# Loading the first element's blocks four rows to a partition, with its turned blocks written by Pool's queue

## The chip, the cores and the metric

The kernel runs on one core of one Trainium2 chip. The metric is the device time of one execution in microseconds, lower is better. TensorE (PE) multiplies matrices, VectorE (DVE) and ScalarE (ACT) work elementwise, GpSimd (POOL) does elementwise work in on-chip memory (SBUF), and transfers between SBUF and DRAM are issued by SP, ACT or Pool.

## The reference

Two layers over x of shape (8, 256, 96, 96), fp32. Each is a group norm, an operation and a residual.

```
# layer 0, on xn = groupnorm(x), per element b
q_f, k_f, v_f = fft2(w1 xn + b1), fft2(w2 xn + b2), fft2(w3 xn + b3)
attn = normalize(q_f) @ normalize(k_f)^T * temperature     # 8 heads of 32 channels, over 9216 frequencies
attn = softmax(real(attn)) + 1j * softmax(imag(attn))
x = x + w_out @ abs(ifft2(attn @ v_f))
# layer 1, on xn = groupnorm(x)
q, k, v = softplus(Wq xn + bq), softplus(Wk xn + bk), Wv xn + bv
x = x + (q @ (k^T v)) / (q @ sum(k))
```

## The kernel before

The Fourier transforms are not computed. What the attention of layer 0 needs of x are channel-by-channel sums of even and odd combinations of pixels with their mirror images, and the imaginary part of attn acts on an image that is mirrored and rotated along a table R. For each of the eight elements the program has these stages:

- **pair sums** (`pair_sums`): a row h of the image is paired with its mirror row. For 48 rows in 12 units (u = 0 to 11) of four rows each (G = 4), and a thirteenth for the middle row, `turn_blocks(u)` brings channels into the free dimension with DVE's 32x32 stream transposes, `pair(u)` makes sums and differences (tile eo), and `products` multiplies these on PE into two accumulators (acc), 24 matmuls a unit.
- **attention** (`attention`): a chain of small steps that makes the matrix mz.
- **rotation** (`rotate`): 49 steps that multiply the turned rows by pieces of R and write the result y. Its inputs come back from DRAM: xtd (turned blocks) and rx (R).
- **images** (`images`) forms the complex image, its absolute value, and the output projection; **layer1** and **output** do layer 1.

In the program the stages of element b are woven with the pair sums, the attention and the rotation of element b + 1, so that PE always has work. Only element 0 has nothing to be woven with: its pair sums start when the program starts. Its loop is at the end of the kernel:

```python
        for i, _ in enumerate(sums):
            if i > 3:
                next(parts, None)
            if i > 20 and i % 2 == 0:
                fetch()
            if i > 26:
                next(turns)
```

A pair-sum unit yields once per third of its products, so i is 1 + 3u + q. `parts` is the generator `tables`, which builds R and then the small constants, `fetch` loads one row pair of xtd (and R's piece where a new one begins), `turns` makes one rotation step.

The order on each engine is written by hand: within the manual schedule, the instructions of PE, DVE, Pool, SP and ACT run in the order in which the program emits them. Semaphores carry the data dependencies. The transfers of SP and ACT share eight completion lanes, in turn: a transfer also waits until the one eight before it on its lane is complete.

Memory: two arenas of 128 partitions x 2 channel halves (k) x 9232 floats take turns as x (`x_of(b)`) and y (`y_of(b)`). While the pair sums of element b run, its x arena holds no x yet but stages blocks. `load_grouped(b, v)` loads block v (0 to 5, two units each; 6 is the middle row): 32 channels of a group times four sets of two rows on 128 partitions, f the rows and g their mirror rows, in half k = v % 2; eight transfers of 192 KB, with one cut in two for block 0. `turn_blocks(u)` transposes f (unit 2v + r uses the r-th row) and the reversed g into the turned buffer, which begins at TO in both halves. After the second unit of a block it issues on SP the write of the turned block (1.5 MB) to xtd and then the load of block v + 2 (L372 and the lines after it). There is one turned buffer. At r = 0 two small copies (L364, L365) move a column of g by one row, the wrap.

`tables` writes 96 rows of a cosine table to DRAM (rt), reads them back as the long rows of R in 384-byte pieces (`big`, L270), and writes R to rx cut into 13 pieces with overlapping ends (L279, L280), from which `load_r` (L608) fetches one piece per four rows.

Of the kernel before, what the change touches and what calls it, by code (L numbers as in the profile page):

```python
# [52 lines left out]
F32 = mybir.dt.float32  # L53
# [4 lines left out]
P = 128  # L58
# [4 lines left out]
TR = 4  # L63
# [10 lines left out]
def two_layer_kernel(ctx: ExitStack, tc: tile.TileContext, x, w1t, b1, w2t, b2, w3, b3, wot, temp,  # L74
# [49 lines left out]

    SG = NB8 * 2 * W
    TO = 2 * SG + 4

    def staged(b, v, at=0):

        return x_of(b)[:, v % 2, at * SG:at * SG + SG + at]  # L130

    def turned(b):

        return [x_of(b)[:, c, TO:TO + 2 * NQ * C].rearrange("p (q r n) -> p q r n", q=NQ, r=2) for c in range(2)]

    def load_grouped(b, v):

        xs = x[b].rearrange("(c i) h w -> i c h w", i=32)
        if 2 * v == NG:
            m = H // 2  # L140
            f, g = (staged(b, v, i)[:, 0:C].rearrange("p (c w) -> p c w", c=NB8) for i in range(2))
            for q in range(NQ):
                s = slice(32 * q, 32 * q + 32)
                n = 32 if q else 31
                o = W + 1 - 32 * (q + 1)
                nc.sync.dma_start(out=f[s], in_=xs[:, :, m, s])
                nc.sync.dma_start(out=g[s, :, 0:n], in_=xs[:, :, m, o:o + n])
            return
        f, g = (staged(b, v, i)[:, 0:SG].rearrange("p (c w) -> p c w", c=NB8) for i in range(2))
        for a in range(G):  # L150
            h, s = 2 * (G * v + a), slice(32 * a, 32 * a + 32)
            nc.sync.dma_start(out=f[s], in_=xs[:, :, h:h + 2].rearrange("p c r w -> p c (r w)"))
            if h:
                nc.sync.dma_start(out=g[s], in_=xs[:, :, H - h - 1:H - h + 1].rearrange("p c r w -> p c (r w)"))
            else:
                nc.sync.dma_start(out=g[s, :, 0:W], in_=xs[:, :, H - 1])
                nc.sync.dma_start(out=g[s, :, W:2 * W], in_=xs[:, :, 0])

    setup = y_of(0)[:, 0, :]
    t0 = setup[0:H, 0:6 * W]  # L160
    nc.scalar.dma_start(out=t0[:, 0:2 * W], in_=tmat[0, :, W:3 * W])
    for v in range(2):
        load_grouped(0, v)


    ident = const.tile([P, P], F32, name="ident")
# [22 lines left out]
    nc.scalar.dma_start(out=gavg_sb, in_=gavg)  # L189
    gri = setup[:, 6 * W:6 * W + 2 * P]  # L190
    nc.scalar.dma_start(out=gri, in_=gmat)

    pw = const.tile([P, 1], F32, name="pw")
    nc.vector.memset(pw, 1.0)
# [49 lines left out]
    rt = dram.tile([H, 2 * W], F32, name="rt")  # L244
    NP = NG
    RW = TR * (W + 2) + P - W
    rx = dram.tile([NP + 1, W, RW], F32, name="rx")

    xtd = dram.tile([2, NG // 2, P, 2 * NQ * C], F32, name="xtd")
    xtm = dram.tile([W, C], F32, name="xtm")  # L250
# [1 line left out]
    def tables():  # L252

        pcs = ps_tile("pcs")
        for c in range(2):
            nc.tensor.matmul(pcs[0:H, c:c + 1], lhsT=csn[0:1, c, :], rhs=ones[0:1, 0:1], start=True, stop=True)
        cs = t0[:, 5 * W:5 * W + 2]
        nc.vector.tensor_copy(cs, pcs[0:H, 0:2])
        r0 = t0[:, 2 * W:3 * W]
        nc.vector.tensor_scalar_mul(t0[:, 0:W], t0[:, 0:W], cs[:, 0:1])  # L260
        nc.vector.scalar_tensor_tensor(r0, in0=t0[:, W:2 * W], scalar=cs[:, 1:2], in1=t0[:, 0:W], op0=ALU.mult, op1=ALU.add)
        for i in range(2):
            o = (3 + i) * W
            nc.vector.tensor_copy(t0[:, o:o + 1], r0[:, 0:1])
            nc.vector.tensor_copy(t0[:, o + 1:o + W], r0[:, W - 1:0:-1])
        nc.scalar.dma_start(out=rt, in_=t0[:, 3 * W:5 * W])
        big = y_of(0)[0:W, 1, 0:(N + 1) * (W + 2) + P - W]
        rows = big[:, 0:(N + 1) * (W + 2)].rearrange("p (r w) -> p r w", r=N + 1)
        v = rt[0:N + 1, 1:]
        nc.scalar.dma_start(out=rows[:, :, 1:W + 1], in_=bass.AP(v.tensor, v.offset, [[1, W], [2 * W, N + 1], [1, W]]))  # L270
        nc.scalar.copy(rows[:, :, 0:1], csn[0:W, 2, 0:N + 1].unsqueeze(2))
        nc.scalar.mul(rows[:, :, W + 1:W + 2], csn[0:W, 2, 0:N + 1].unsqueeze(2), -1.0)
        nc.scalar.copy(big[:, (N + 1) * (W + 2):], csn[0:W, 2, 0:P - W])
        yield
        for q in range(NQ):
            s = slice(32 * q, 32 * q + 32)
            v = big[s, 0:NP * TR * (W + 2)]
            src = bass.AP(v.tensor, v.offset, [list(v.ap[0]), [TR * (W + 2), NP], [1, RW]])
            nc.scalar.dma_start(out=rx[0:NP].rearrange("i (j q) w -> q j i w", q=NQ)[q], in_=src)  # L279
        nc.scalar.dma_start(out=rx[NP][:, 0:P + 2], in_=big[:, N * (W + 2):N * (W + 2) + P + 2])  # L280
        yield
        for j in range(4):
            o = HEAD * j
            nc.vector.tensor_copy(gsel[:, 0:16, j], gri[:, o:o + 16])
            nc.vector.tensor_copy(gsel[:, 17:32, j], gri[:, P + o + 1:P + o + 16])
            nc.vector.tensor_copy(gsel[:, 32, j:j + 1], gri[:, o + 16:o + 17])
        nc.vector.reduce_sum(rep4[:, 0:D], ident.rearrange("p (j d) -> p d j", d=D), axis=AX.X)
        for j in range(1, 4):
            nc.vector.tensor_copy(rep4[:, 32 * j:32 * j + 32], rep4[:, 0:D])
        nc.vector.tensor_copy(sel8.rearrange("p (i d) -> p i d", d=D), rep4[:, 0:8].unsqueeze(2).to_broadcast([P, 8, D]))  # L290
        nc.vector.tensor_scalar_mul(csn[:, 0:2, N + 1:H], csn[:, 0:2, N + 1:H], -1.0)
        yield from load_small()
# [42 lines left out]
    def pair_sums(b):  # L335
# [9 lines left out]
                                     rhs=eo[0:np_, q, c, m * (P + 1):C + 1 + m], start=(first and m == 0), stop=last,  # L345
                                     skip_group_check=True)

        wrap = two.tile([P, 2 * NB8], F32, tag="wrap", name=f"wrap_{b}")

        def turn_blocks(u):  # L350

            v, r = divmod(u, 2)
            t = turned(b)
            if u == NG:
                f, g = (staged(b, v, i)[0:W, 0:C].rearrange("p (c w) -> p c w", c=NB8) for i in range(2))
                nc.vector.tensor_copy(g[0:32, :, 31:32], f[0:32, :, 0:1])
                for i, src in enumerate((f, g[:, :, ::-1])):
                    nc.vector.transpose(out=t[i][0:W, 0, 0].rearrange("p (c i) -> p c i", c=NB8), in_=src)
                nc.sync.dma_start(out=xtm, in_=t[0][0:W, 0, 0])
                return  # L360
            f = staged(b, v, 0).rearrange("p (c r w) -> p c r w", c=NB8, r=2)
            if r == 0:
                g = staged(b, v, 1)
                nc.vector.tensor_copy(wrap, g[:, 0:SG:W])  # L364
                nc.vector.tensor_copy(g[:, W:SG + 1:W], wrap)  # L365
            o = SG + (1 - r) * W + 1
            g = x_of(b)[:, v % 2, o:o + SG].rearrange("p (c n) -> p c n", c=NB8)[:, :, W - 1::-1]
            for i, src in enumerate((f[:, :, r], g)):
                nc.vector.transpose(out=t[i][:, :, r].rearrange("p q (c i) -> p q c i", c=NB8),  # L369
                                    in_=src.rearrange("p c (q w) -> p q c w", q=NQ))  # L370
            if r:
                nc.sync.dma_start(out=xtd[:, v].rearrange("c p m -> p c m"), in_=x_of(b)[:, :, TO:TO + 2 * NQ * C])  # L372
                if v + 2 <= NG // 2:
                    load_grouped(b, v + 2)

        def pair(u):

            eo = ring_tile(f"eo_{b}_{u}").rearrange("p (q c n) -> p q c n", q=NQ, c=2)
            nq, np_ = (NQ, P) if u < NG else (1, W)
            ft, gt = (t[0:np_, 0:nq, u % 2] for t in turned(b))  # L380
            e, o = (eo[0:np_, 0:nq, c, 1:C + 1] for c in range(2))
            nc.gpsimd.memset(eo[0:np_, 0:nq, :, 0:CB:CB - 1], 1.0 if u < NG else R2)  # L382
            if u == 0:
# [215 lines left out]
    def rotate(b):  # L599
# [5 lines left out]
        def load_r(i):  # L605
            tm = tm_tile(f"tm_{b}_{i}")
            o = (TR if i < NP else 1) * (W + 2) + P - W
            nc.sync.dma_start(out=tm[:, 0:o], in_=rx[i][:, 0:o])  # L608
            return tm

        order = [(c, h, h // TR) for h in range(0, N, 2) for c in range(2)] + [(0, N, NP)]
        area = x_of(b)
        slots = [area[0:W, k, o + 4 * C * i:o + 4 * C * (i + 1)].rearrange("p (c m) -> p c m", c=2)
                 for k, o, n in ((0, LO, 3), (1, LO, 3), (0, LO + 12 * C, 1)) for i in range(n)]
        assert LO + 16 * C <= AW and LO + 12 * C <= LO + NS * CH + 2 * CH
        xts, tms = {}, {}
        at_ = [0]
# [1 line left out]
        def fetch():  # L619
# [9 lines left out]
            if h == N:  # L629
                nc.sync.dma_start(out=xts[i][:, 0, 0:C], in_=xtm)  # L630
            else:
                v, a = divmod(i, G)
                nc.sync.dma_start(out=xts[i], in_=xtd[:, v, 32 * a:32 * a + 32].rearrange("c j (q m) -> (j q) c m", q=NQ))

        def step(i):
# [20 lines left out]
        def steps():  # L656

            for i in range(len(order)):
                while at_[0] < min(i // 2 + len(slots) - 1, len(order) // 2 + 1):
                    fetch()  # L660
                step(i)
                if i >= 24 and i % 8 == 0 and i // 8 < 6:
                    load_x(b, i // 8 - 3)
                yield

        return fetch, steps()

# [347 lines left out]
    with tc.manual_schedule(engines={E.PE, E.DVE, E.Pool, E.SP, E.Activation}):  # L1015
# [1 line left out]
        next(parts)  # L1017
        fetch, turns = rotate(0)
        for i, _ in enumerate(sums):
            if i > 3:  # L1020
                next(parts, None)
            if i > 20 and i % 2 == 0:
                fetch()
            if i > 26:
                next(turns)
        finish(mix(0, attention(0), turns))
        for b in range(B):
# [60 lines left out]
```

## Time and profile before

| | us |
|---|---|
| median of 3 runs | 2651.48 (2646.25 to 2654.46) |
| profiled execution | 2650.85 |
| its span, first to last instruction | 2649.0 |
| PE busy | 2509.3 (95%) |
| DVE, ACT, POOL busy | 1789.0, 1155.9, 865.6 |
| mean granted PE clock | 0.984 |
| pair-sum products of element 0, first to last | 16.0 to 127.7 |
| first image product of element 0 (L710) | 180.31 |

The page gives busy times and, in 40 slices of 66 us, busy tenths of each engine. PE's busy time counts pipelined matmuls, so that a full PE says that matmuls followed one another, not that the array was at its peak. A wait line reads: engine, line and tile that waited, "<-", what ended the wait, then the total in us, how often, and the longest. A line of the order of time reads: start, duration, engine, line, operation, tiles, count, and in brackets the idle time before it with what ended it. SPq and ACTq are the DMA-issuing parts of SP and ACT; the duration of an issue is not that of the transfer.

### The profile page before, as it was taken

What the parts mean: (1) busy time and instruction counts of PE and PEld (TensorE: products, weight loads), DVE (VectorE), ACT (ScalarE), POOL (GpSimd) and SP (SyncE); (2) the same over time, 40 slices, a digit from 0 to 9 for tenths busy, and PEclk for the clock granted to TensorE, in tenths of its full rate; (3) what the DMA queues carried; (4) which work ended last, traced back from release to release, by engine and by line L of the source; (5) the groups of instructions that cost most, each with busy time, mean ns of one, the idle gap of its engine ahead of it and who ended that gap; (6) DMA issues with size and microseconds to landing.
All of it is one profiled execution on the core that took longest, in us unless ns stands there. A gap on an engine that the chain in (4) does not pass through costs nothing. (4 is left out here: it accounts for less than half of the span.)

```text
span 2649.0 us, 41157 instructions
## 1 busy us (share of the span) xinstructions
PE 2509.3 (95%) x15580; PEld 1730.2 (65%) x15580; DVE 1789.0 (68%) x3449; ACT 1155.9 (44%) x1985; POOL 865.6 (33%) x817
## 2 busy tenths in 40 slices
PE   3799999999999999999999999999999999999987
PEld 3775666757677576766668566685666757667544
DVE  3457866577756777568675686757866678766766
ACT  0035353453634526344353544435354353534554
POOL 2213514136042451324422343223523135141311
PEclk8899999999999999999999999999999999999999
DMA  9872628637195461935629264492636826286003
GB/s 210 238 216 60 166 71 270 205 67 189 40 313 161 106 173 57 315 120 143 153 90 305 80 167 129 159 316 42 166 89 230 245 60 179 58 289 210 1 7 144
DMA packets 282797, 413.27 MB, mean 156 GB/s; under 512 B 40772, under 2 KB 208872, under 8 KB 282600
## 3 DMA queue, kind: packets, MB, share of 16 engines
q1 hardware_dynamic: 274304, 406.16, 53.2%
q10 hardware_dynamic: 8296, 4.49, 0.8%
q8 instruction: 123, 2.02, 0.3%
q14 instruction: 74, 0.61, 0.1%
HBM read 256.72 MB, written 153.86 MB: 155 GB/s over the span
## 5 line engine op out<-in xcount | busy, mean ns | idle before, releaser
L710 PE MATMUL z<-arena,mz 128*128 128x384 f32 (+1 forms) x2304 | 593.4, 491 | 0.0
L718 PE MATMUL po<-e,wo 128*128 128x384 f32 x1536 | 527.6, 487 | 1.7 <-ACT e L755 1.7
L754 POOL TENSOR_TENSOR e<-e 128x768 f32<-128x768 f32 x192 | 348.4, 1815 | 552.7 <-ACT e L753 529.3
L343 PE MATMUL acc<-eo 128*128 128x257 f32 (+2 forms) x2368 | 437.1, 336 | 50.0 <-POOL eo L382 23.0
L343 PEld LDWEIGHTS acc<-eo 128*128 128x128 f32 (+1 forms) x2368 | 383.8, 194 | 143.9 <-issue 42.4
L710 PEld LDWEIGHTS z<-arena,mz 128*128 128x128 f32 (+1 forms) x2304 | 310.5, 164 | 236.0 <-issue 51.9
L718 PEld LDWEIGHTS po<-e,wo 128*128 128x128 f32 x1536 | 290.0, 190 | 204.7 <-ACT e L755 7.2
L749 DVE TENSOR_TENSOR e<-z,xT 128x768 f32<-128x768 f32 x384 | 361.9, 950 | 75.4 <-PE z L710 74.9
L647 PEld LDWEIGHTS y<-tm,arena 96*128 96x128 f32 x3072 | 365.9, 195 | 52.9 <-issue 18.9
L647 PE MATMUL y<-tm,arena 96*128 96x128 f32 x3072 | 385.7, 281 | 15.3 <-DMA arena<-xtd 6.4
L753 ACT ACTIVATE e<-e 128x1536 f32<-128x1536 f32 x192 | 284.5, 1482 | 195.2 <-DVE e L749 193.3
L391 POOL TENSOR_TENSOR eo<-arena 128x768 f32<-128x768 f32 x88 | 184.5, 2096 | 536.3 <-DVE arena L369 473.2
L720 DVE TENSOR_TENSOR arena<-arena,po 128x384 f32<-128x384 f32 x384 | 209.9, 553 | 190.0 <-PE po L718 190.0
L755 ACT ACTIVATE e<-e 128x768 f32<-128x768 f32 x192 | 162.0, 844 | 367.1 <-POOL e L754 363.2
L986 POOL TENSOR_TENSOR arena<-arena,po 128x384 f32<-128x384 f32 x180 | 179.1, 1014 | 224.0 <-ACT po L985 224.0
L369 DVE STREAM_TRANSPOSE arena<-arena 128x768 f32<-128x768 f32 x192 | 175.7, 953 | 32.5 <-DMA xtd<-arena 23.0
L299 DVE BATCH_NORM_STATS2 st<-arena 128x6 f32<-128x384 f32 x384 | 194.4, 548 | 0.0
L654 ACT COPY ys<-y 128x4 f32<-128x4 f32 (+1 forms) x200 | 32.4, 162 | 363.8 <-DVE arena L653 363.7
L878 PE MATMUL xT<-ident,arena 128*128 128x128 f32 x1152 | 148.4, 277 | 10.0 <-ACT xT L881 9.6
L878 PEld LDWEIGHTS xT<-ident,arena 128*128 128x128 f32 x1152 | 127.2, 142 | 32.0 <-issue 13.6
L985 ACT COPY po<-o 128x384 f32<-128x384 f32 x180 | 79.0, 485 | 157.4 <-PE o L977 152.4
L653 DVE COPY arena<-y 128x384 f32<-128x384 f32 (+1 forms) x200 | 109.1, 546 | 40.8 <-PE y L647 38.6
(225 smaller groups left out, 2493.1 us busy)
## 6 DMA issues: line engine op xcount, KB each, us to landing
xtd<-arena SPq DMA_DIRECT2D x48, 1536.0 KB
arena<-xtd SPq DMA_DIRECT2D x192, 384.0 KB
arena<-in_x_dram SPq DMA_DIRECT2D x96, 768.0 KB
out_dram<-arena SPq DMA_DIRECT2D x192, 384.0 KB
arena<-in_x_dram SPq DMA_DIRECT2D x376, 192.0 KB
tm<-rx SPq DMA_DIRECT2D x96, 159.0 KB
wl<-in_w1t_dram SPq DMA_DIRECT2D x8, 256.0 KB
wl<-in_w2t_dram SPq DMA_DIRECT2D x8, 256.0 KB
```

The costliest lines, as they stand in the source:

```text
L299: nc.vector.bn_stats(out=st[:, k, c, :], in_=x_of(b)[:, k, c * CH:(c + 1) * CH])
L343: nc.tensor.matmul(acc[c][:, m * (C + 1):m * (C + 1) + C + 1 - m * P], lhsT=eo[0:np_, q, c, 1 + m * P:1 + (m + 1) * P], rhs=eo[0:np_, q, c ...
L391: nc.gpsimd.tensor_add(e, ft, gt)
L647: nc.tensor.matmul(pu[:, o:o + P], lhsT=xt[:, s, k * P:(k + 1) * P], rhs=tm[:, n:n + P], start=True, stop=True)
L710: nc.tensor.matmul(out[:, 0:CH].rearrange("p (h q) -> p h q", q=PR), lhsT=columns(mz, k, c, j), rhs=yz[:, k, f, :, o:o + PR], start=(k == ...
L718: nc.tensor.matmul(po[:, 0:CH], lhsT=wo[:, k, m * P:(m + 1) * P], rhs=e[:, k, :], start=(k == 0), stop=(k == KC - 1))
L720: nc.vector.tensor_add(x[:, m, n], x[:, m, n], po[:, 0:CH])
L749: nc.vector.tensor_add(e[:, 2 * c:2 * c + 2, :].rearrange("p t (q h) -> p t q h", h=H), pz[:, 0:CH].rearrange("p (h q) -> p q h", h=H).uns ...
L753: nc.scalar.activation(e, e, AF.Square)
L754: nc.gpsimd.tensor_add(e[:, 0:2, :], e[:, 0:2, :], e[:, 2:4, :])
L878: nc.tensor.transpose(pt[:, j * C + k * P:j * C + (k + 1) * P], x[:, k, o:o + P], ident)
L986: nc.gpsimd.tensor_add(x[:, m, r], x[:, m, r], t)
```

## The change

For element 0 alone (all others keep their way):

- a block group is four rows of x per partition: three groups (v = 0, 2, 4) of eight 384 KB transfers instead of six blocks of eight 192 KB. Groups 0 and 1 are staged in the two halves of the x arena, group 2 in half 0 of the y arena, the middle row in half 1 of it. All three groups are loaded ahead of everything else; the middle row is loaded after unit 9.
- the turned blocks have two places, T4 and T4 + 2*NQ*C, used in turn by v, and the write to xtd is issued by Pool instead of SP.
- R is written to DRAM in 96 long rows (and a small tile rxm for the last piece); `load_r` reads its piece out of the long rows.
- the parts of `tables` are drawn at i = 1, 6 and from 7 on, instead of from 4 on; the fetches begin at i = 18 instead of 22 and the rotation steps at i = 29 instead of 27.
- the eight places of the fetched rows lie under the staged groups (there were seven, elsewhere in the arena); x for the images' third piece, load_x(0, 2), is loaded after the rotation instead of at its step 40.

```diff
+    S4 = 2 * SG
+    T4 = 2 * S4 + 4
+    def part_of(b, v, o, n):
+        if b:
+            return x_of(b)[:, v % 2, o:o + n]
+        if 2 * v == NG:
+            return y_of(b)[:, 1, H // 2 * W + H // 4 * HB + o:H // 2 * W + H // 4 * HB + o + n]
+        V = v // 2
+        return x_of(b)[:, V, o:o + n] if V < 2 else y_of(b)[:, 0, 10 * W + o:10 * W + o + n]
+    def turned(b, v):
+        o = TO if b else T4 + v % 2 * 2 * NQ * C
+        return x_of(b)[:, :, o:o + 2 * NQ * C]
...
-            h, s = 2 * (G * v + a), slice(32 * a, 32 * a + 32)
-            nc.sync.dma_start(out=f[s], in_=xs[:, :, h:h + 2].rearrange("p c r w -> p c (r w)"))
+            h, s = 2 * G * v + n * a, slice(32 * a, 32 * a + 32)
+            nc.sync.dma_start(out=f[s], in_=xs[:, :, h:h + n].rearrange("p c r w -> p c (r w)"))
...
-    for v in range(2):
-        load_grouped(0, v)
+    load_grouped(0, 0)
...
+    for v in (2, 4):
+        load_grouped(0, v)
...
-    rx = dram.tile([NP + 1, W, RW], F32, name="rx")
+    rx = dram.tile([W, RL], F32, name="rx")
+    rxm = dram.tile([W, P + 2], F32, name="rxm")
...
+        yield
-        big = y_of(0)[0:W, 1, 0:(N + 1) * (W + 2) + P - W]
+        big = y_of(0)[0:W, 1, 0:RL]
...
-            nc.scalar.dma_start(out=rx[0:NP].rearrange("i (j q) w -> q j i w", q=NQ)[q], in_=src)
-        nc.scalar.dma_start(out=rx[NP][:, 0:P + 2], in_=big[:, N * (W + 2):N * (W + 2) + P + 2])
+            nc.scalar.dma_start(out=rx.rearrange("(j q) w -> q j w", q=NQ)[q], in_=big[32 * q:32 * q + 32])
+        nc.scalar.dma_start(out=rxm, in_=big[:, N * (W + 2):N * (W + 2) + P + 2])
...
-            if r:
-                nc.sync.dma_start(out=xtd[:, v].rearrange("c p m -> p c m"), in_=x_of(b)[:, :, TO:TO + 2 * NQ * C])
-                if v + 2 <= NG // 2:
+            if u % 2:
+                (nc.sync if b else nc.gpsimd).dma_start(out=xtd[:, v].rearrange("c p m -> p c m"), in_=turned(b, v))
+                if b and v + 2 <= NG // 2 or v + 2 == NG // 2:
                     load_grouped(b, v + 2)
...
+        places = ((0, LO, 3), (1, LO, 3), (0, LO + 12 * C, 1)) if b else ((0, T4 - 16 * C, 4), (1, T4 - 16 * C, 4))
...
-                v, a = divmod(i, G)
+                v, a = divmod(i, G) if b else (i // 8 * 2 + i % 2, i % 8 // 2)
...
-                if i >= 24 and i % 8 == 0 and i // 8 < 6:
+                if i >= 24 and i % 8 == 0 and i // 8 < 6 and (b or i < 40):
                     load_x(b, i // 8 - 3)
                 yield
+            if b == 0:
+                load_x(b, 2)
...
-            if i > 3:
+            if i in (1, 6) or i > 6:
                 next(parts, None)
-            if i > 20 and i % 2 == 0:
+            if i > 17 and i % 2 == 0:
                 fetch()
-            if i > 26:
+            if i > 28:
                 next(turns)
```

## The prediction

> **What bounds the kernel now.** I read the page's slices first, then the busy time by window, then the waits, and last the order of time of the first 110 us. The page shows where time can be had at all:
>
> ```profile
> PE   3799999999999999999999999999999999999987
> ...
> PEclk8899999999999999999999999999999999999999
> ```
>
> TensorE is full from the third slice on (a slice is 66 us); only the first two have holes, and there the granted clock is 0.8. All that the diff touches for element 0 runs in these two slices. The same in windows of 20 us (columns: window, length, PE, weight load, DVE, ACT, POOL busy with counts, granted clock, DMA share, GB/s):
>
> ```profile
> 0.00:20.00 20.00, 4.75 (x16) 4.14 (x17) 9.77 (x39) 2.05 (x5) 4.24 (x62) 1.00 1.02 191
> 20.00:40.00 20.00, 9.80 (x48) 8.54 (x47) 8.12 (x24) 0.00 (x0) 6.31 (x7) 0.78 1.11 287
> 40.00:60.00 20.00, 7.13 (x40) 6.29 (x38) 3.70 (x8) 0.00 (x0) 0.39 (x1) 0.76 0.52 159
> 60.00:80.00 20.00, 10.84 (x52) 9.53 (x53) 9.10 (x12) 0.00 (x0) 8.59 (x7) 0.76 0.97 215
> 80.00:100.00 20.00, 15.74 (x81) 14.00 (x81) 6.22 (x10) 0.00 (x0) 6.87 (x6) 0.84 0.86 228
> ...
> 120.00:140.00 20.00, 19.56 (x155) 18.02 (x155) 8.93 (x33) 5.94 (x18) 0.58 (x1) 1.00 0.94 262
> ```
>
> PE works 48.3 of the first 100 us and is full after 107. The waits up to 110 us say what it lacks:
>
> ```profile
> POOL eo L391 <- DVE arena L369: 78.5, 9, 20.6
> ...
> DVE wrap L364 <- DMA arena<-in_x_dram: 20.9, 5, 6.0
> DVE arena L369 <- DMA xtd<-arena: 20.4, 4, 7.4
> DVE wrap L364 <- DMA wo<-in_wot_dram: 12.4, 1, 12.4
> ```
>
> PE waits for eo, Pool (which makes it) for the transposes of L369, and these for two transfers: the x blocks (20.9, and the 12.4 put down to wo, where the blocks were late as well) and the write of the turned blocks to xtd (20.4). The order of time shows the cycle, one per two rows of blocks:
>
> ```profile
> 51.97 0.38 SPq L372 DMA_DIRECT2D xtd<-arena  x1
> ...
> 57.63 1.84 DVE L369 STREAM_TRANSPOSE arena<-arena 128x768 f32<-128x768 f32 x2 [3.79 <-DMA xtd<-arena]
> ...
> 74.14 1.84 DVE L369 STREAM_TRANSPOSE arena<-arena 128x768 f32<-128x768 f32 x2 [6.05 <-DMA xtd<-arena]
> ...
> 85.01 1.84 DVE L369 STREAM_TRANSPOSE arena<-arena 128x768 f32<-128x768 f32 x2 [3.12 <-DMA xtd<-arena]
> ```
>
> Turns 0, 2, 4, 6, 8, 10 start at 12.15, 32.10, 57.63, 74.14, 85.01 and 103.59. From the issue of the write before each to its first transposes passed 7.8, 5.7, 6.5, 6.2 and 6.4 us: a write costs about 6.5 us, and no turn starts while it is in flight.
>
> **What the Trainium skill says.** "DMA: Bandwidth & Descriptors", section Anatomy of one DMA, prices a DMA issued by Pool at 2.0 us + bytes/436 GB/s: an estimate of 2.0 + 1.57 MB/436 = 5.6 us alone. The SP writes here took 5.7 to 7.8, which agrees; the kernel before has no Pool DMA. The same page, section Issuing engines are not separate DMA queues: all queues run on the same 16 DMA engines and interleave, so Pool's queue adds no bandwidth. The trace agrees in that the page's DMA share stands at 1.0 to 1.1 in the first 40 us. "SBUF — State Buffer", section SBUF: two separate sides, warns that DVE copies can keep Pool from writing the descriptors; no run here shows it yet. "TensorE: Matmul & The Clock Gate", Part 1: an array that idles falls back to half clock. Here 24 products took 5.2 us after a pause and 4.2 to 4.4 in full flow, so PE gaps cost a little twice.
>
> **The change part by part.**
>
> *Loads.* The 49 block loads of 192 KB (two of 96) become 25 transfers of 384 KB (one split into 288 and 96), three groups of 3.1 MB, none of which waits for a buffer to be turned. "At once" is not what SP will do: SP and ACT share eight completion lanes, and a transfer waits for the one that had its lane eight before. In the compiled order of the changed kernel the first load of group 1 waits for the long rows of R to be read (arena<-rt), and two later ones for the writes of rx; in the kernel before those landed at about 28 us and 38 us. Group 0: the window row gives 191 GB/s; 3.1 MB + 0.3 MB of tables at that rate is 18 us. I take 17.5 (15 to 20), against 11.77 now: 5.7 us lost at the start. Group 1: until it is in, x 6.3 MB, tables and R 4.1 MB, one write and part of the next, about 2.5 MB, must move: 13 MB, 3.8 of it in 20 us, the rest at 287 GB/s in 32 us: 52; the finest slices show up to 350, so I take 49 (43 to 54). Group 2 needs 3.1 MB and two writes more, 6.3 MB at 250: 74.
>
> *Two buffers and Pool's queue.* That the turned blocks have two buffers would let turn 2v start while the write v-1 is in flight. But one tile holds both channel halves, and the write takes both; in the compiled order the transposes of turns 2, 4, 6, 8 and 10 each still carry a wait for the write of the pair before (turn 2 for write 0, turn 4 for write 1, and so on), the odd pairs in the first of two transposes, the even in the second, which gives back only 0.9 us. So the cycle stays: two turns with the subtraction between them (32.10 to 36.75: 4.65 us), then a write W. W from below is 5.6 (the skill's price) and from above twice what I take, 17, since nothing here shows Pool's descriptors beside DVE. I take 9 while the x groups are still coming and 8.5 after, 2 us over the SP writes for the sharing. Queued behind each Pool issue is the memset and add of the next odd pair; Pool has 26.2 us of adds in 100, so an issue of 1 to 2 us is hidden by PE's 4.3 us per pair. SP loses six writes and 24 loads of about 0.4 us each: no gain, its waits are for data.
>
> *The sum for the turns.* Turn 0 at 17.5 + 0.35 for the wrap. From wrap to the end of turn 1 it takes 6.94 now (11.77 to 18.71): 24.4. Turn 2 at 24.4 + 9 = 33.4; pair done 38.1, write landed 47; turn 4 at 49 + 0.4 = 49.4; turn 6 at 49.4 + 4.65 + 8.5 = 62.6; turn 8 at 76 with its wrap; turn 10 at 89.4. Now it is 103.6: 14 us earlier. After turn 10 PE is full in both kernels with the same work, so this goes to the end, except for the next.
>
> *Rotation.* It starts at sum 29 instead of 27. Two steps of eight 128x128 products that PE now runs in the hole before turn 10 (97.1 to 99.2) fall into the full part: 2 x 1.06 = 2.1 us lost. The fetches of xtd wait more: the fifth carries waits for the writes 2 to 4, the seventh for write 5. With turn 11 ending near 94 write 5 lands at 103, and the seventh fetch (step 12) at 107; PE reaches step 12 after turn 10 + 20 us = 109 (in the kernel before turn 10 to step 12 took about as long). Priced at 0, up to 4 if PE gets there first.
>
> *R in long rows, the shift of the table work, load_x(0, 2) after the rotation, the wrap of 32 columns:* rx in rows of 19 KB instead of 1.7 KB saves at most some of ACT's 7.6 us of issue, ahead of the first need of tm by over 40 us. The 12 copies and the small memory work are DVE's 3 us in time in which it waits. load_x(0, 2) lands about 5 us after the rotation; its first reader is the fifth projection, 25 to 30 us after, and the DMA queues are at 0 GB/s from 200 to 240 us. If that cover were gone it would cost its 4 us. All at 0.
>
> Sum: 14 - 2.1, rounded to 12. The profiled execution took 2650.85 (span 2649.0 and 1.85 around it), 0.6 below the median 2651.48. 2650.85 - 12 = 2638.9; I say **2639**.
>
> **The rivals.** (a) *The two buffers and the early loads work nearly as the words say*: W near 6.5 and group 1 by 43. Then turn 4 at 43.4, turn 10 at 43.4 + 3 x 11.5 = 78, 25.6 - 2.1 = 23 us: 2628. For: the SP writes took 6.5 with transfers beside them. Against: the waits in the compiled order, and the shared engines. (b) *The loads are no earlier, because the lanes and bandwidth set them*: group 1 at 56, W 9: turn 10 at 56.4 + 41 = 97, gain 4: 2647. For: 25 us of x, R and writes are asked for in the first 50, at 287 GB/s. (c) *Slower: Pool's write is long.* Five writes lie in the chain. Turn 10 = 24.4 + 5W + 4 x 4.65 + about 1 = 44 + 5W; equal to now where this is 101.5, so from W = 11.5 on it is slower. With W = 15, turn 10 is at 119 and the end 17 later: 2668. For: the descriptors are written by Pool while it also has the adds and DVE the transposes, all queues share the engines. Against: the price of 5.6, and DVE is idle while it waits. (d) *The change moves nothing*, because another wait ends last (the R rows late for the first rotation): 2651; little speaks for it, tm has over 40 us.
>
> **How the numbers follow.** Case of the forecast (gain 8 to 18) 0.45, (a) 0.18, (b) with (d) 0.22, (c) 0.15. A measurement of this kernel can tell about 0.3% from no change, 8 us. The forecast and (a) count as faster: 0.63. (b), (d) as the same, and of (c) a little: 0.23. Slower: 0.14. The range takes in (a) and (b): 2626 to 2651; (c) is left out with the tail of (a), 2 in 10.
>
> **What would show it.** Right: turn 10 near 89; the transposes of even turns waiting for xtd<-arena each time, 7 to 10 us after Pool's issue; turn 4 waiting for x near 49; PE full from about 94 and the first z product near 168 instead of 180.3. Wrong: no wait of L389 for the writes (two buffers do overlap); even turns more than 16 us apart (Pool's write dear); a PE wait for xtd near step 12; any change after 200 us.

## The result, and the profile after

The changed kernel takes 2659.55 us (median, 2649.92 to 2667.09), the kernel before 2653.6 beside it: a ratio of 1.0012, 95% interval 0.9989 to 1.0035. No change can be told, where 2639 was forecast.

The profiled execution took 2667.09 us (span 2665.3), 16 above the one of before. Of these, 6.7 are there when the first image product of element 0 starts (187.0 against 180.3), 7.0 more when the last image product of the program does (2554.3 against 2540.6), and the rest after it. In the middle part the granted clock differs between the two executions (0.90 against 0.98 from 400 to 500 us); over a whole execution its mean goes from 0.972 to 0.988 for the kernel before alone. What the change does is over when TensorE (PE) starts the image products of element 0, so the start of the first one is the sharp measure here. It is read from one profiled execution of each kernel, so that a difference of one or two us says little. The order of time of that line, PE alone, from 130 to 200 us, before (L710) and in the changed kernel (L733); counts, durations in ns, first and last start, forms:

```profile
L710 PE MATMUL z<-arena,mz x67: 486/486/590, 180.3 to 199.8; 128*128 128x384 f32 x35, 128*32 128x384 f32 x32
L733 PE MATMUL z<-arena,mz x56: 485/486/590, 187.0 to 197.2; 128*32 128x384 f32 x32, 128*128 128x384 f32 x24
```

187.0: 6.7 us later than before, not 12 earlier. In the time that would be a ratio of 1.0025, inside the interval. The page's slices, TensorE and its clock:

```profile
PE   2899999999999999999999999999999999999988
...
PEclk7999998999999999999999999999999999999987
```

In the first two slices PE went from 3 and 7 to 2 and 8; from the third on it is as full as before. The windows say where in the first the time is (columns as before: PE, weight load, DVE, ACT, POOL busy, clock, DMA share, GB/s):

```profile
20.00:40.00 20.00, 5.83 (x24) 5.00 (x24) 6.04 (x7) 0.00 (x0) 0.00 (x0) 0.84 1.02 227
40.00:60.00 20.00, 4.88 (x14) 4.13 (x15) 0.96 (x1) 0.00 (x0) 3.71 (x4) 0.50 1.10 227
60.00:80.00 20.00, 13.88 (x69) 12.12 (x68) 14.22 (x32) 0.00 (x0) 10.38 (x10) 0.80 0.48 158
```

From 20 to 60 us PE works 10.7 us (before 16.9), Pool nothing at all for 20 us, and the DMA engines are full. What Pool waited for stands at the top of the waits up to 110 us:

```profile
POOL xtd L392 <- DMA arena<-in_x_dram: 47.7, 1, 47.7
...
PE acc L363 <- POOL eo L402: 25.7, 1, 25.7
DVE arena L389 <- DMA xtd<-arena: 21.2, 3, 9.7
```

One wait of 47.7 us, the last 25.1 of them after its data was there: the **write** of turned blocks (L392, to DRAM) was held until **loads** of x had landed. The order of time puts the pieces in a row (L389 is the transposes, L402 the memset of eo, L363 the products):

```profile
24.39 1.83 DVE L389 STREAM_TRANSPOSE arena<-arena 128x768 f32<-128x768 f32 x2
...
51.33 0.95 POOL L392 DMA_DIRECT2D xtd<-arena  x1 [47.69 <-DMA arena<-in_x_dram]
52.28 0.14 POOL L402 MEMSET eo<- 128x12 f32 x1
...
55.12 7.11 PE L363 MATMUL acc<-eo 128*128 128x257 f32 x24 [25.73 <-POOL eo L402]
...
63.09 1.84 DVE L389 STREAM_TRANSPOSE arena<-arena 128x768 f32<-128x768 f32 x2 [9.68 <-DMA xtd<-arena]
...
73.61 1.84 DVE L389 STREAM_TRANSPOSE arena<-arena 128x768 f32<-128x768 f32 x2
```

Turn 1 ended at 26.2, so its write had its data from then on. It was issued at 51.33, when group 1 was in. Queued behind it on Pool were the memset and add of unit 1, whose data was there too; so PE stood from 29.4 to 55.1, and turn 2 waited for the write until 63.1.

The write of a whole pair is one access over both channel halves of the x arena, from T4 in half 0 to T4 + 1536 in half 1. Group 1 is staged in half 1, at a place the access steps over but its span covers. In the compiled order of the changed kernel write 0 carries a wait for DVE and for seven of the eight completion lanes of SP and ACT.

### The profile page after: what moved, and what is told of

Its sections match the earlier page's. It is cut to its first block, busy times and chain, and to the rows that moved or that the text cites. A ratio compares the mean times of both kernels' runs of the same rounds, so it can differ in the third digit from the quotient of the medians.

```text
span 2665.3 us, 41107 instructions
## 1 busy us (share of the span) xinstructions
PE 2520.2 (95%) x15580; PEld 1743.0 (65%) x15580; DVE 1790.9 (67%) x3443; ACT 1155.7 (43%) x1985; POOL 872.7 (33%) x823
## 5 line engine op out<-in xcount | busy, mean ns | idle before, releaser
L733 PE MATMUL z<-arena,mz 128*128 128x384 f32 (+1 forms) x2304 | 593.8, 492 | 0.0
L363 PE MATMUL acc<-eo 128*128 128x257 f32 (+2 forms) x2368 | 436.2, 336 | 66.7 <-POOL eo L402 25.7
L363 PEld LDWEIGHTS acc<-eo 128*128 128x128 f32 (+1 forms) x2368 | 383.3, 194 | 160.2 <-issue 49.9
L733 PEld LDWEIGHTS z<-arena,mz 128*128 128x128 f32 (+1 forms) x2304 | 311.3, 165 | 235.6 <-issue 52.0
L743 DVE TENSOR_TENSOR arena<-arena,po 128x384 f32<-128x384 f32 x384 | 209.9, 553 | 189.4 <-PE po L741 189.4
L389 DVE STREAM_TRANSPOSE arena<-arena 128x768 f32<-128x768 f32 x192 | 175.8, 953 | 31.5 <-DMA xtd<-arena 30.1
```

The lines of the kernel that those rows point to most:

```text
L363: nc.tensor.matmul(acc[c][:, m * (C + 1):m * (C + 1) + C + 1 - m * P], lhsT=eo[0:np_, q, c, 1 + m * P:1 + (m + 1) * P], rhs=eo[0:np_, q, c ...
L733: nc.tensor.matmul(out[:, 0:CH].rearrange("p (h q) -> p h q", q=PR), lhsT=columns(mz, k, c, j), rhs=yz[:, k, f, :, o:o + PR], start=(k == ...
L743: nc.vector.tensor_add(x[:, m, n], x[:, m, n], po[:, 0:CH])
```

## The experiments

Starts of turns (turn u is the transposes of unit u; two numbers where its two transposes stand apart) and of the first image product in us, from one profiled execution of each kernel, and the ratio of times to the kernel before with its 95% interval (20 runs or more, but 12 of the changed kernel, 14 of e3_small_late and 6 of e10_small_pool):

| kernel | turn 2 | turn 4 | turn 10 | first image product | ratio |
|---|---|---|---|---|---|
| before | 32.1 | 57.6 | 103.6 | 180.3 | 1 |
| changed | 63.1 | 73.6 | 113.4 | 187.0 | 1.0012 [0.9989, 1.0035] |
| e1_split | 27.9 | 64.8 | 94.2 | 173.6 | 0.9976 [0.9961, 0.9992] |
| e2_before_split | 27.1 / 45.0 | 65.0 | 102.8 | 179.4 | 0.9993 [0.9976, 1.0009] |
| e3_small_late | 65.0 | 73.7 | 108.6 | 186.8 | 1.0003 [0.9985, 1.0020] |
| e4_split_late | 28.2 | 60.6 | 98.2 | 177.2 | 0.9978 [0.9962, 0.9994] |
| e5_before_pool | 33.1 | 52.4 | 108.0 | 189.4 | 1.0024 [1.0006, 1.0041] |
| e6_split_last | 28.0 | 59.3 | 84.0 | 172.8 | 0.9975 [0.9958, 0.9991] |
| e7_big_pool | 27.9 | 61.8 | 86.4 | 175.9 | 0.9976 [0.9962, 0.9990] |
| e8_sp_writes | 27.3 | 67.4 | 87.6 | 180.3 | one time, 2643.25 |
| e9_split_rest | 63.7 | 74.2 | 101.2 | 179.9 | 0.9993 [0.9979, 1.0007] |
| e10_small_pool | 36.6 | 62.5 | 87.4 | 163.8 | 0.9914 [0.9887, 0.9940] |
| e11_r_later | 38.0 | 46.8 | 88.7 | 167.8 | 0.9970 [0.9956, 0.9984] |
| e12_before_small | 43.8 | 57.6 | 104.0 | 179.7 | 1.0005 [0.9990, 1.0019] |

### e1_split and e2_before_split: is the span of the write the cause?

e1_split is the changed kernel with each write of element 0 as two transfers, one per channel half. Nothing else moves, and the same bytes go to the same places:

```diff
-                (nc.sync if b else nc.gpsimd).dma_start(out=xtd[:, v].rearrange("c p m -> p c m"), in_=turned(b, v))
+                if b:
+                    nc.sync.dma_start(out=xtd[:, v].rearrange("c p m -> p c m"), in_=turned(b, v))
+                else:
+                    for c in range(2):
+                        nc.gpsimd.dma_start(out=xtd[c, v], in_=turned(b, v)[:, c])
```

> The changed kernel, but each write of turned blocks to xtd is two transfers from Pool's queue, one per channel half, so that in the compiled order write 0 no longer waits for the loads of group 1, nor a turn for the write just before it. Theory A (Pool's first write, and Pool's adds queued behind it, waited 47.7 us for group 1, because one access over both halves spans the staged group): write 0 is issued near 26 us instead of 51, turn 2 starts near 28 instead of 63, turn 4 when group 1 is in, near 51 instead of 73.6; turn 10 near 80 instead of 113, the first image product near 157 instead of 187.0, the time 25 to 32 us below the changed kernel. Theory B (Pool's write itself is slow, or the loads set the pace anyway): turn 10 stays within 5 us of 113 and the first image product within 5 us of 187.

e2_before_split cuts the write of the kernel before (on SP) in the same way.

> The kernel before, with the SP write of element 0's turned blocks as two transfers, one per half; nothing else. Theory A says that the kernel before paid the same wait in small: write 0 was issued at 24.3 though turn 1 ended at 18.7. Expected: write 0 near 19, turn 2 near 27 instead of 32, turn 10 some 5 us before 103.6, first image product near 175 instead of 180.3, the time 3 to 8 us lower. Theory B: no difference beyond 2 us in the first image product.

Order of time of e1_split, transposes and Pool's writes:

```profile
24.21 1.83 DVE L389 STREAM_TRANSPOSE arena<-arena 128x768 f32<-128x768 f32 x2
...
25.49 1.40 POOL L396 DMA_DIRECT2D xtd<-arena  x2 [21.85 <-DVE arena L389]
...
27.92 1.83 DVE L389 STREAM_TRANSPOSE arena<-arena 128x768 f32<-128x768 f32 x2
...
64.75 1.84 DVE L389 STREAM_TRANSPOSE arena<-arena 128x768 f32<-128x768 f32 x2
```

The write now waits for DVE alone and leaves as its turn ends, at 25.5 instead of 51.3, and turn 2 follows with no wait. So the hold was a dependency by span, not by data. The waits of turns for the write before are gone as well: with one half per access, the two buffers work. The first image product came 13.4 us earlier than in the changed kernel, at 173.6; 157 was expected. Group 1 of x was in only at 64.3 instead of 51.3. Two writes were now in flight beside it, and the last three of its loads left only at 45.4, 52.7 and 60.1, two of them after SP had stood 6.9 and 7.1 us for lanes of small loads (bkq and wo).

In the kernel before the split gave nothing. The first half of its first write did leave earlier (18.45 instead of 24.26), but SP then stood 16.3 us for a lane that a write of rx had, before it could issue the second half, and turn 2's second transposes waited for that until 45.0.

### e9_split_rest: how much is the hold, how much the waits of turns for writes?

The changed kernel with writes 0 and 1 whole and only writes 2 to 5 split (`if b or v < 2:` ahead of the whole write).

> Edit: the changed kernel with writes 0 and 1 of element 0 whole, and writes 2 to 5 in two, one per half of the channels. It tells the price of the first wait (write 0 kept until group 1 of x is in) from the price of the waits of turns for the write before. Theory A (the first wait is most of the loss): write 0 still issued at about 51 us, turn 2 at about 63, turn 4 at about 74 as in the changed kernel; then turn 6 at about 80 with no wait, turns 8 and 10 when group 2 is in, about 93 and 100 (changed kernel: 113 for turn 10); first product of the image matmuls at 176 to 180 (changed kernel 187.0, all writes split 173.6). Rival B (the waits for the write before are the loss, the first wait is covered by later ones): first product at about 173.6, as with all writes split. Times within 0.3% of the kernel before in both cases.

Its order of time:

```profile
52.19 0.96 POOL L393 DMA_DIRECT2D xtd<-arena  x1 [48.54 <-DMA arena<-in_x_dram]
...
63.70 1.84 DVE L389 STREAM_TRANSPOSE arena<-arena 128x768 f32<-128x768 f32 x2 [9.43 <-DMA xtd<-arena]
...
74.23 1.84 DVE L389 STREAM_TRANSPOSE arena<-arena 128x768 f32<-128x768 f32 x2
...
80.90 1.83 DVE L389 STREAM_TRANSPOSE arena<-arena 128x768 f32<-128x768 f32 x2
```

Turn 6 starts at 80.9 without a wait (changed kernel 85.7), turn 10 at 101.2. First image product 179.9. So of the 13.4 us that e1_split gains, 7.1 are the waits of later turns for the write before, and 6.3 the hold of write 0, with the wait of turn 2 for that write in it. (This is one order of taking them away; the kernel with writes 0 and 1 split and the others whole was not run.) A hold of 25 us was worth only 6, because without it the turns wait for x: in e1_split turn 4 until 64.3 and turn 8 until 87.1. The numbers are those of Theory A, but "most of the loss" is not right as put: it is half.

### e5_before_pool and e8_sp_writes: what is Pool's queue worth?

e5_before_pool is the kernel before with the writes of element 0 issued by Pool (one line: `(nc.sync if b else nc.gpsimd)`), e8_sp_writes is e6_split_last (below) with the writes issued by SP.

> The kernel before, with the one edit that element 0's writes to xtd are issued by Pool; one buffer, blocks of two rows, whole writes. Gives the price of a Pool write, W, apart from the rest, and shows the false wait in its smaller form. Expected: W from issue to the next transposes 7 to 9 us (SP's: 5.7 to 7.8). Write 0 waits for the loads of block 1 as in the kernel before, now with Pool's adds queued behind it: the first eo of Pool moves from 18.9 to 24 us or later, write 1 no longer stands 15 us behind loads on SP. First image product within 5 us of 180.3, either way.

> As the first of this set, with the halves' writes on SP's queue instead of Pool's: they stand behind all loads of the three groups there. Tells what Pool's queue is worth once the false wait is gone. Expected: turn 2 still near 28 (it needs no write), turn 4 when write 0 has landed behind the loads, near 65 instead of 51, turn 10 near 85 to 90; first image product 5 to 12 us after that with Pool's queue. If Pool's queue is worth nothing, within 2 us of it.

Alone, Pool's queue costs: the first product came 9.1 us later. Pool stood at writes 0, 2 and 4 for loads of x (6.4, 11.5 and 8.2 us beyond the end of the turn), with the adds behind them. With the split and the early loads it pays 7.5 us (172.8 against 180.3): on SP the first two writes queued behind the loads of x and left from 53.3 us on, and turn 4 waited 15.6 us for them. So here moving the write off SP paid only where the write itself waits for nothing but its turn. Group 1 was in at 51.3 here, with no write in flight, as in the changed kernel. The wrap copy of turn 4, which waits for it, in e8_sp_writes and then in e6_split_last, where Pool's writes were in flight:

```profile
51.32 0.19 DVE L385 COPY wrap<-arena 128x32 f32<-128x32 f32 x1 [18.38 <-DMA arena<-in_x_dram]
```

```profile
58.92 0.19 DVE L385 COPY wrap<-arena 128x32 f32<-128x32 f32 x1 [24.18 <-DMA arena<-in_x_dram]
```

### e3_small_late and e4_split_late: the small loads

In the changed kernel SP's own waits up to 110 us say why group 2 was late:

```profile
SPq L173 <- DMA b<-in_b_dram: 27.2, 1, 27.2
SPq L171 <- DMA arena<-rt: 16.8, 1, 16.8
SPq L173 <- DMA wo<-in_wot_dram: 7.3, 1, 7.3
```

Loads of x stood for a lane taken by the biases (b, which themselves waited for a memset on the held Pool) and by wo. e3_small_late draws the small loads later (`i in (1, 6) or i > 17`), e4_split_late does so beside the split.

> The changed kernel, but the parts of the tables after the second (DVE's copies and ACT's small loads) are drawn from i = 18 on instead of 7, so that the completion lanes of group 2's loads no longer follow ACT's small loads. Write 0 still waits for group 1. Theory C (group 2 was late because SP stood 27 us behind the load of b and 13 behind those of wo): turn 8 has its data, no wait for x there, and starts at about 97 with turn 10 near 107 instead of 113; first image product near 181. Theory A says the rest of the loss stays: turn 2 near 63 as in the changed kernel. If group 2 was not late in fact, nothing moves.

> Both edits: writes in two halves, and the small loads drawn from i = 18 on. Theory A with C: turn 2 near 28, turn 4 near 51, turn 6 near 60, group 2 in by 65, turn 10 near 78 and the first image product near 153, the time 30 us below the changed kernel and 24 below the kernel before. Theory B: as the changed kernel within 5 us.

A later place is no better. e3 was 5 us earlier at turn 10 and gave it back by the image products (186.8): write 5 then stood 6.6 us on Pool for a fetch of xtd, with an add behind it, and PE waited 2.7 and 1.8 us more for eo. In e4 turn 8 waited until 91.5; SP had again stood for b, 21.9 us. The small loads still lay among those of x.

### e6_split_last and e7_big_pool: no small load among the loads of x

e6_split_last is e1_split with `i > 30` and `finish(parts)` ahead of the attention. e7_big_pool also lets Pool issue the read-back of R ahead of the sums.

> Writes in halves (as in the first of these), and the tables' third part on (DVE's copies and ACT's small loads) drawn only from i = 31 on and finished before the attention, so that in the compiled order no load of x follows a small load on its completion lane. What remains ahead of group 1 on its lanes is the read-back of R (arena<-rt) and the three writes of rx. Theory D (the loads of groups 1 and 2 were held by lanes that ACT's small loads had): group 1 is in near 51 us as in the changed kernel, not 60 to 64; group 2 near 62, not 87 to 91; turn 4 near 51, turn 6 near 58, turn 8 near 65, turn 10 near 76; first image product near 155 to 160, against 173.6 with the halves alone. Theory E (the DMA engines were simply full): group 1 still near 60 and turn 10 near 94.

> As the one before, and the read-back of R (arena<-rt, 384-byte pieces) is issued by Pool at the start, so that it holds none of the completion lanes; the loads of group 1 then do not wait for it (16.7 us of SP's wait in the changed kernel). Theory D: group 1's loads begin near 12 us instead of 28.8, its last ones still follow two rx writes, so it is in near 45 instead of 51; turn 4 near 45, turn 10 near 71. Theory E: the bytes are the same, group 1 stays near 51. A rival: Pool takes long to write the 4704 pieces, and write 0 and the adds queue behind it: turn 0's products and turn 2 later than 28.

In e6 group 2 no longer waits behind a small load: turn 10 at 84.0 instead of 94.2. But group 1 was in at 58.9, not at 51, with the DMA engines full: taking the small loads out of its way is not enough. In e7, with R's read-back on another queue, it was in at 61.5; SP stood 27.2 us there for a lane that a write of rx had, so e7 only exchanged one wait for another. And the 10 us of turn 10 did not reach the image products. Windows of e6:

```profile
80.00:100.00 20.00, 20.00 (x139) 18.72 (x138) 11.95 (x34) 0.81 (x4) 11.56 (x13) 1.00 1.02 325
100.00:120.00 20.00, 12.50 (x85) 11.40 (x83) 5.53 (x19) 2.61 (x8) 0.58 (x1) 0.82 0.76 187
```

PE is full from 80 on and then has a hole of 7.5 us. ACT issues the small loads, and this late its queue also holds copies of the rotation's results (L678, L679):

```profile
95.25 4.48 ACTq L236 DMA_DIRECT2D b<-in_b_dram  x4
...
99.83 0.48 ACT L678 COPY arena<-y 128x384 f32<-128x384 f32 x1 [4.48 <-DMA b<-in_b_dram]
```

This copy reads nothing of b; it stood behind the issues of b. Five more waits of this kind, 1.9 to 3.7 us each, follow behind bkq, tcol and wo, and DVE and PE waited for the copies. It is the fault of write 0 once more, on another queue: what waits in a queue holds whatever stands behind it.

### e10_small_pool: small loads early and on another queue

e1_split with all these small loads issued by Pool and drawn ahead of the sums (and with them the rest of `tables`).

```diff
-            nc.scalar.dma_start(out=bkq4[:, c:c + 1], in_=bass.AP(v.tensor, v.offset, [[0, 4], [1, 32], [1, 1]]))
+            nc.gpsimd.dma_start(out=bkq4[:, c:c + 1], in_=bass.AP(v.tensor, v.offset, [[0, 4], [1, 32], [1, 1]]))
...
-        next(parts)
+        finish(parts)
         fetch, turns = rotate(0)
         for i, _ in enumerate(sums):
-            if i in (1, 6) or i > 6:
-                next(parts, None)
```

> Edit: the changed kernel with element 0's writes split per half of the channels, and all the small loads (biases, temperatures, query and key weights, wo) issued by Pool's queue and drawn before the sums, so that no load of x on SP's queue stands behind a small load's completion. Theory D (group 2 was late because its loads stood in the queue behind the small loads): turn 4 when group 1 is in, about 59; group 2 in by about 77, turn 10 at about 84 (split alone: 94.2) and first product of the image matmuls at 162 to 166 (split alone: 173.6), time 8 to 14 us below the kernel before. Rival E (the DMA engines are full from 20 to 60 us, the order doesn't matter): turn 10 no earlier than 92 and first product at 171 to 175. Possible cost in both: Pool issues some 14 small loads between 4 and 27 us, which may delay its sums of unit 1 and write 0 by some us.

The best version: 2634.93 us (six runs), ratio 0.9914 [0.9887, 0.9940]. Its first image product and two waits of its turns for x, from the order of time:

```profile
L737 PE MATMUL z<-arena,mz x90: 486/486/847, 163.8 to 199.8; 128*128 128x384 f32 x58, 128*32 128x384 f32 x32
```

```profile
62.09 0.19 DVE L385 COPY wrap<-arena 128x32 f32<-128x32 f32 x1 [18.72 <-DMA arena<-in_x_dram]
...
80.27 0.19 DVE L385 COPY wrap<-arena 128x32 f32<-128x32 f32 x1 [4.41 <-DMA arena<-in_x_dram]
```

163.8 as expected, 9.8 us ahead of e1_split, with groups and turns some 3 us later than I had said. The time is lower by more than the 8 to 14 us expected: 0.9914 is 23 us, its interval 16 to 30, and the first product's 16.5 lie in it. Pool's issues do delay turn 2, to 36.6, and this costs nothing, because turn 4 waits for group 1 until 62.1 anyway. SP stood 19.2 us for the lane of R's read-back before the first load of group 1 left at 32.2, and the DMA engines were full all that time. The transfers of e10 from 20 to 40 us and from 40 to 62 us:

```profile
DMA packets 5879, 3.99 MB, mean 200 GB/s; under 512 B 5132, under 2 KB 5811, under 8 KB 5816
```

```profile
DMA packets 2741, 6.75 MB, mean 307 GB/s; under 512 B 220, under 2 KB 2194, under 8 KB 2706
```

While R is read back (384-byte pieces) most packets are short and the engines move 200 GB/s; afterwards 307. The Trainium skill, "DMA: Bandwidth & Descriptors", section Specifications, says that a transfer needs at least 512 B to run at line rate. The trace agrees in direction; no run separates the share of the short pieces from that of other traffic.

### e11_r_later and e12_before_small

e11_r_later: as e10, with R's read-back on SP between the loads of group 1 and group 2.

> Edit: as e10_small_pool, and R's read-back into the long rows is issued by SP's queue after group 1's loads of x and before group 2's, so that group 1 doesn't wait for R's write to HBM. Theory F (group 1 is late because its first load stands behind R's write and read-back and shares the DMA engines with it): group 1 in by 33 to 40, turn 4 by 36 to 42, group 2 in by about 60 to 66, turn 10 at 66 to 74, first product of the image matmuls at 147 to 156, time 20 to 30 us below the kernel before. Rival G (the chain of R ends last once the first element's turns are early: R's sums and transposes come later on Pool and TensorE and set the start of the spectral products): turn 10 moves as said, but the first product stays at 160 to 166.

```profile
46.77 1.84 DVE L388 STREAM_TRANSPOSE arena<-arena 128x768 f32<-128x768 f32 x2
...
81.64 0.19 DVE L384 COPY wrap<-arena 128x32 f32<-128x32 f32 x1 [21.49 <-DMA arena<-xtd]
```

Turn 4 starts at 46.8, 15.7 us earlier than in e10, and turn 8 at 82.1, 1.4 later: it waited 21.5 us. (The releaser named is a fetch of xtd. What the copy reads is group 2, whose last load left at 65.6, with R's read-back and the writes of rx ahead of it; that this was what it lacked is inferred.) Neither theory holds: the order of the loads decides which group is late, but not when the last one is in. The DMA share is 1.0 or more in every window of 20 us from 20 to 100 us in both kernels, so that here what must be moved seems to be the bound.

e12_before_small: the kernel before with e10's move of the small loads alone.

> Edit: the kernel before, with only the move of the small loads (biases, temperatures, query and key weights, wo) from ACT's queue to Pool's, all drawn before the sums. It tells whether the gain of e10_small_pool (0.9914, first product of the image matmuls at 163.8) needs the changed kernel's staging and writes, or lies in the small loads alone. Theory H (the kernel before is held by its own turns: each pair waits for the write of the pair before and, two groups on, for loads that wait for those turns): turn 10 at 95 or later (before 103.6), first product at 172 to 180 (before 180.3), time within 0.3% of the kernel before or up to 8 us below. Rival I (its turns were late because SP's queue stood behind the small loads): turn 10 by 90, first product by 166, time 12 us or more below the kernel before, like e10_small_pool.

First product 179.7, turn 10 at 104.0: Theory H. Its turns wait for the write before, 29.5 us in five waits. So neither mend does anything for the kernel before (e2, e12), and the change gains 6 us with the first alone and 23 with both: writes that wait only for their turn, and loads of x with no small load's lane among them. The kernel before with both mends, and the changed kernel with the second alone, were not run.

## Why the prediction was wrong

**The step that failed** is "Queued behind each Pool issue is the memset and add of the next odd pair ... so an issue of 1 to 2 us is hidden", with the sum that follows from it, "Turn 2 at 24.4 + 9 = 33.4". I priced how long the issue takes (0.95 us measured for write 0, 0.74 for the others: right) and put at nothing what the issuing instruction waits for. Write 0 waited 25.1 us past the end of turn 1. In the compiled order I read the waits of the turns and not those of the write. The profile before had shown the same hold in small: its write 0 left at 24.26, though turn 1 ended at 18.71, and SP's waits up to 130 us put 16.9 us of L372 down to loads of x.

```profile
16.88 1.83 DVE L369 STREAM_TRANSPOSE arena<-arena 128x768 f32<-128x768 f32 x2
...
24.26 0.40 SPq L372 DMA_DIRECT2D xtd<-arena  x1
```

```profile
SPq L372 <- DMA arena<-in_x_dram: 16.9, 9, 7.3
```

On SP only transfers stood behind it; on Pool the adds did, and PE with them.

**The arithmetic of the miss.** Turn 2 came at 63.1 instead of 33.4, 29.7 late: 1.8 because group 0 was in later (turn 1 ended at 26.2, not 24.4), 25.1 for the hold, and 2.8 because this first write took 11.8 and not 9. From turn 2 to turn 10 took 50.3 against a predicted 56.0 (5.7 better), from turn 10 to the first image product 73.6 against 78.6 (5.0 better). 29.7 - 5.7 - 5.0 = 19.0 is just the distance from the forecast 168 to 187.0.

The hold is not all of it. In e1_split it is gone, and so are the waits of the even turns, which the forecast had kept; still the first image product comes at 173.6, not 168, and the time is 6 us below the kernel before, not 12. What is left lies in the arrival of x, below.

**Right: the cost of Pool's write.** I took 9 and 8.5 us. From Pool's issue to the next transposes that needed it passed 11.8, 5.6, 7.2, 11.0 and 7.6 us, a mean of 8.6 (the second an upper bound, as no wait is shown). The profile's page gives 7.4 from issue to landing as the median of six, where the skill's formula in "DMA: Bandwidth & Descriptors", section Anatomy of one DMA, gave an estimate of 5.6; 5.6 was the best one. (Of the five SP writes that the forecast read, the last, 6.4 us, ended by the trace with a load of x, not with the write; the other four, 5.7 to 7.8, carry the reading.) So rival (c) is not what happened: its decision point, W = 11.5 for all five, was not reached.

**Right: the wait of even turns stays** while a write is one access over both halves (9.7, 5.3, 6.3 and 5.8 us in the changed kernel), and goes when it is two (e1_split, e9_split_rest). It is worth 7.1 us.

**Half right: group 1 by 49.** It was in at 51.3, but only because the write that should have run beside it was held. With the writes in flight, and the loads in this order, it was 58.9 to 64.3. The term mis-sized is the rate. The 13 MB of the forecast by 49 us ask for 317 GB/s after 20 us; from 20 us until group 1 was in, the traces show 220 in the changed kernel, 224 in e1_split and 269 in e6_split_last. I took it from the one full window of the kernel before, 20 to 40 us at 287, and from its finest slices, as if it were a rate that the engines give to any mixture of transfers.

**Wrong: group 2 by 74.** Even with the hold gone it was late: turn 8 started at 87.6 in e1_split, because loads of x stood for lanes taken by small loads: group 2 left only behind the last loads of group 1, from 64.5 on. I had named the lanes of R for group 1 and not those of the small loads. Without these it was in at 76.9 (e6_split_last) and 80.3 (e10_small_pool).

**Not separately tested:** the two rotation steps moved (2.1 us; the trace of before has one of them from 97.1 to 99.2 and the next only from 101.5), R in long rows, and load_x(0, 2). Nothing in the waits up to 130 us points to the first two, and PE's waits from 185 to 300 us name no load of x.

**What stays open.** In e10_small_pool and e11_r_later the first products differ by 4 us, the ratios by 0.0056, some 15 us; e10's interval alone spans 14. Of the profiled executions, the last image product starts 15 us apart (2526.6 and 2541.6), so that 11 of them arise after the first; what they are wasn't traced down.

## What to carry to other kernels

When a transfer is moved to another engine's queue, read what that transfer waits for before asking what it costs to issue: everything behind it on the new queue inherits the wait, as the adds did on Pool and the copies on ACT. An access with a gap in it may be ordered against whatever lies in the gap; two accesses without gaps can be cheaper than one. And when a stall goes, look up at once what is late next: here it was the write, then the small loads' lanes, then the DMA engines themselves.

## What the runs showed of the hardware

- The issue of one transfer can take SP long: in e11_r_later the load of x issued next after R's read-back of 4704 pieces took 20.66 us, where the loads issued up to 20.4 us had taken 0.3 to 0.5 each.
- Pool's issue is cheap even for many pieces: 0.74 us for a 1.5 MB write, 1.1 for the same in two, and 2.12 us for the 4704 pieces of R (e7_big_pool). The Trainium skill, "SBUF — State Buffer", section SBUF: two separate sides, warns of DVE copies holding up Pool's descriptors; no run here shows such a delay, or tells it from the sharing of the DMA engines.
- Two writes of 1.5 MB in flight beside the loads moved the arrival of 3.1 MB of x by some 8 us: group 1 was in at 51.3 in e8_sp_writes and at 58.9 in e6_split_last, which differ only in the queue of the writes (one profiled execution of each). In e1_split, with the small loads among those of x, it was 64.3.
